# Block 0's first loads of an adapter and FFN kernel: x's first four k as two loads on two queues, B and A ahead of the rest of x

## The chip, the cores and the metric

The kernel runs on one core of a Trainium2 chip. The metric is the time of one execution on the device in microseconds (us), as the median of several runs. Engines are called by their names in the profile: PE (TensorE's products), PEld (its weight loads), DVE (VectorE), ACT (ScalarE), POOL (GpSimd) and SP (SyncE). SP does no arithmetic here. It issues most of the DMAs. ACTq and SPq are the queues of instructions of ScalarE and SyncE, in which register loads and DMA issues stand too.

## The reference

```python
def reference(x, ids, A, B, gate_w, up_w, down_w, ...):   # x: 8 x 256 x 1024
    Bx  = einsum('bni,bri->bnr', x, B[ids])               # rank 16, one adapter per batch row
    y   = einsum('bnr,bor->bno', Bx, A[ids])              # 8 x 256 x 1024
    q   = fp8(clip(y / in_scale)) * in_scale              # the same for gate and up
    h   = silu(q @ gate_w.T) * (q @ up_w.T)               # 2752 wide
    return x + fp8_linear(h, down_w)                      # back to 1024
```

x goes through a low-rank adapter that is picked by an index for each of the 8 batch rows, then through a feed-forward layer whose inputs are rounded to fp8, and is added at the end.

## The kernel before

The 2,048 tokens are worked on as four blocks t of 512 (two batch rows each), tokens along the free dimension. The 1,024 features of x are eight groups k of 128 partitions. x lies in memory in pieces, as `PIECES` says for each block: for block 0 the first piece holds k 0 to 3, the second k 4 to 6 and the third k 7, and each piece is one load (`load_x(t, k)`, line 378). Later blocks 2 and 3 come as one piece.

The head of the kernel is what the change touches. For block 0 TensorE does, in this order (lines 633 to 638):

- `pass_time(warm, 16, TB)`: 16 products of zeros, which need no load;
- `two_times_b(0, ...)`: Bx, tile `bx`, 8 groups k of four products each, with four more products of zeros behind k 3. All four products of a k read x's group k and one of the two adapters' B (tile `b`, two loads, one for each batch row);
- seven more products of zeros, while VectorE and ScalarE copy `bx` to `bm`;
- `two_times_a(0, bm)`: 64 products to the tiles `c`, from A (tile `a`, four loads of 16 rows each) and `bm`. VectorE and ScalarE round them to fp8, tile `xg`;
- `gate_up(0, 0, ...)`: the products `y` of the first chunk of 128 hidden features, from `xg` and the first chunk of weights (tile `w_gu`, 1 MB a chunk, the first as two halves). From here on products follow one another to the end: 22 chunks for four blocks, then the way back (`yd`).

TensorE's products are pinned in the order of the program (`multiply`, line 469). The adapter chosen for a batch row is a number in memory: `ids_i` is loaded first, and `adapter_of(batch, queue)` reads one number from it into a register of the queue that it names; a load of B or A that uses the number stands behind it on that queue.

All loads of data are issued by SyncE in the order of the program, but for `ids_i` and the first B, which ScalarE issues. In order of the program the loads are: ids; x k 0 to 3; B of batch row 0 (ScalarE); B of row 1; x k 4 to 6; A of row 1 (two loads); A of row 0 (two loads, behind another register load on SyncE); x k 7; five chunks of gate and up weights; then B, x and A of block 1, and B and x of blocks 2 and 3. ScalarE loads its activation table (`preload_act_table`, line 307) right behind the issue of ids.

The completion of each load is counted on a semaphore. The framework deals these out itself, and it adds the waits that follow from using one again.

Of the kernel before, what the change touches and what calls it, by code (L numbers as in the profile page):

```python
# [14 lines left out]
AF = mybir.ActivationFunctionType  # L15
# [10 lines left out]
NH = H // P  # L26
# [9 lines left out]

KS = NH // 2

PIECES = ((4, 3, 1), (4, 3, 1), (NH,), (NH,))
FP8_MAX = 448.0  # L40

SAME_MAX = 240.0
# [17 lines left out]
def x_of(x4, t, k):  # L60

    first = 0
    for n in PIECES[t]:
        if k < first + n:
            break
        first += n
    at = (t * NH + first) * P * TB
    piece = x4[at : at + n * P * TB].rearrange("(p k n) -> p k n", p=P, k=n)
    return piece, first
# [214 lines left out]
def adaln_ffn(  # L284
# [13 lines left out]
    nc = tc.nc  # L298
# [5 lines left out]

    ids_i = const.tile([1, NB], I32, name="ids_i")
    nc.scalar.dma_start(out=ids_i, in_=ids)
    nc.scalar.preload_act_table(AF.Silu)
    zeros = const.tile([P, TB], BF16, name="zeros")
    nc.vector.memset(zeros, 0.0)  # L309
    ones = const.tile([P, P], BF16, name="ones")  # L310
# [26 lines left out]
    with ExitStack() as fast:  # L337
# [5 lines left out]
        xs = [acts.tile([P, NH, TB], F32, name=f"x{t}") for t in range(NTB)]  # L343
# [8 lines left out]
        b_two = [lora.tile([P, 2 * BROW + R], F32, name=f"b{t}") for t in range(2)]  # L352
# [9 lines left out]
        def adapter_of(batch, queue):  # L362
            return queue.value_load(ids_i[0:1, batch : batch + 1], min_val=0, max_val=7)  # L363

        def load_b(b, i, adapter, queue):
            queue.dma_start(  # L366
                out=b[:, i * BROW : (i + 1) * BROW], in_=b8[bass.ds(adapter * P, P), :]
            )

        def load_a_two(t, j, adapter):  # L370
            for g in range(2):
                row = 32 * (2 * g + j) + R * j
                nc.sync.dma_start(  # L373
                    out=a_two[t][row : row + R],
                    in_=a8[bass.ds(adapter * 2 * R + g * R, R), :],
                )

        def load_x(t, k):
            piece, first = x_of(x4, t, k)
            ks = slice(first, first + piece.shape[1])  # L380
            nc.sync.dma_start(out=xs[t][:, ks, :], in_=piece)  # L381

        w_of = {}

        def load_gate_up(c, parts=1):
# [5 lines left out]
                nc.sync.dma_start(out=w[:, bass.ts(i, n)], in_=src[:, bass.ts(i, n)])  # L391
            w_of[c] = w

        load_x(0, 0)
        load_b(b_two[0], 0, adapter_of(0, nc.scalar), nc.scalar)
        second = adapter_of(1, nc.sync)
        load_b(b_two[0], 1, second, nc.sync)


        load_x(0, 4)  # L400
        load_a_two(0, 1, second)
        load_a_two(0, 0, adapter_of(0, nc.sync))
        load_x(0, 7)
        for c in range(NFIRST):
            load_gate_up(c, parts=1 if c else 2)
        adapters = [adapter_of(2 + q, nc.sync) for q in range(6)]
        for j in range(2):
            load_b(b_two[1], j, adapters[j], nc.sync)
        for k in (0, 4, 7):
            load_x(1, k)  # L410
        for j in range(2):
            load_a_two(1, j, adapters.pop(0))
# [5 lines left out]
        for q in range(4):  # L418
            nc.sync.dma_start(
                out=a_four[32 * q : 32 * q + R], in_=aT[bass.ds(adapters[q] * R, R), :]  # L420
# [309 lines left out]
        for k in range(NH - 1):  # L730
# [23 lines left out]
            first = k % 2 == 0  # L754
# [29 lines left out]
    with found_others.Else():  # L784

        k = NH - 1
# [9 lines left out]
        t, cols = NTB - 1, slice(cut, TB)  # L796
# [88 lines left out]
```

## Time and profile before

| what | value |
|---|---|
| median of 8 runs | 476.45 us (475.70 to 477.22) |
| the profiled execution's own time | 477.99 us |
| its span, first to last instruction | 476.2 us |
| mean granted clock of TensorE | 0.996 |
| TensorE busy | 470.4 us, 99% |
| VectorE, ScalarE busy | 105.6 us, 192.6 us |
| bytes moved by DMA | 53.44 MB, mean 112 GB/s |

The views have these forms. The chain of work that ended last is followed back from the last instruction to what released it, and it is listed in order of time: start, length, what ("issue" is time in which the engine waited for nothing that the profile shows). A timeline line gives start, length, engine, source line, operation, tile written and tiles read, and in brackets the idle time before it with what ended it. A line of the waits gives who waited for whom: total us, times, longest. A line of the windows gives, for a stretch of time, the busy time of each engine, the clock that was granted to TensorE, the share of the DMA engines and the rate. Several products can run beside one another in parts of TensorE's array, so the lengths of products are not summed, and their ends are modelled. When a wait is for several semaphores, the profile names the one that came last.

### The profile page before, as it was taken

How to read it: one execution, taken by the hardware profiler on the slowest of the kernel's cores; microseconds unless marked ns; L12 is line 12 of the kernel's file. 1: busy time of each engine (PE TensorE's matmuls, PEld its weight loads, DVE VectorE, ACT ScalarE, POOL GpSimd, SP SyncE). 2: the span in 40 equal slices, each digit the busy share in tenths (PEclk: the TensorE clock that was granted, in tenths of full speed). 3: DMA queues.
4: the chain of work that ended last, by engine and by line, in shares of the span. 5: the costliest groups of instructions: out<-in, count | busy, mean ns of one | idle time of the engine just before them, and what ended most of it. 6: DMA issues, size and time to landing. Idle time of an engine off the chain costs nothing.

```text
span 476.2 us, 6009 instructions
## 1 busy us (share of the span) xinstructions
PE 470.4 (99%) x2514; PEld 218.5 (46%) x2514; DVE 105.6 (22%) x163; ACT 192.6 (40%) x249; POOL 1.0 (0%) x7
## 2 busy tenths in 40 slices
PE   7999999999999999999999999999999999999997
PEld 4554544444444444444444444444444444444444
DVE  1323332122221212121221212132120121031031
ACT  1323346995556654433455453359212022021000
POOL 0000000000000000000000000000000000000000
PEclk9999999999999999999999999999999999999999
DMA  8996014522222112222201121123335255063031
GB/s 282 400 408 195 1 25 154 178 88 89 88 88 68 32 78 89 89 88 88 88 18 73 44 62 56 61 81 125 101 148 161 61 187 161 17 214 117 3 116 66
DMA packets 13780, 53.44 MB, mean 112 GB/s; under 512 B 1650, under 2 KB 2930, under 8 KB 10674
## 3 DMA queue, kind: packets, MB, share of 16 engines
q1 hardware_dynamic: 13600, 52.92, 32.2%
q8 instruction: 21, 0.34, 0.3%
q14 instruction: 13, 0.11, 0.1%
q10 hardware_dynamic: 146, 0.07, 0.0%
HBM read 44.60 MB, written 8.39 MB: 111 GB/s over the span
## 4 chain that ended last, share of the span: by engine, by line
PE 97%; DMA 1%; SPq 1%; issue 0%; DVE 0%
PE y L470 62%; PE yd L470 31%; PE c L470 2%; PE bx L470 1%; DMA x<-x 1%; SPq L373 0%; DMA ids_i<-ids 0%; SPq L363 0%; PE warm L470 0%; SPq L381 0%; SPq L366 0%; DVE o L695 0%; PE count L470 0%
## 5 line engine op out<-in xcount | busy, mean ns | idle before, releaser
L470 PE MATMUL y<-xg,w_gu 128*128 128x512 fp8e4 x1376 | 298.0, 379 | 0.0
L470 PEld LDWEIGHTS <-w_gu 128*128 128x128 bf16 x1376 | 134.2, 98 | 162.4 <-issue 1.3
L470 PE MATMUL yd<-hid,w_d 128*128 128x512 fp8e4 (+2 forms) x693 | 146.0, 373 | 0.0
L609 ACT ACTIVATE g<-y,gate_s 128x512 f32<-128x512 f32 (+1 forms) x88 | 59.9, 681 | 136.2 <-PE y L470 136.1
L610 DVE SCALAR_TENSOR_TENSOR hid<-y,up_by_down,g 128x512 fp8e4<-128x512 f32 x84 | 63.0, 750 | 219.5 <-PE y L470 161.4
L470 PEld LDWEIGHTS <-w_d 128*128 128x128 bf16 x693 | 66.6, 98 | 78.9 <-issue 1.7
L456 ACT ACTIVATE junk<-w_d 128x1408 bf16<-128x1408 uint16 (+1 forms) x16 | 21.2, 1323 | 88.3 <-DMA w_d<-w_d 88.2
L695 DVE SCALAR_TENSOR_TENSOR o<-yd,down_s,x 128x512 f32<-128x512 f32 x28 | 20.1, 748 | 107.4 <-PE yd L470 93.4
L456 ACT ACTIVATE junk<-w_gu 128x2048 bf16<-128x2048 uint16 (+1 forms) x22 | 41.0, 1864 | 0.0
L463 ACT ACTIVATE junk<-hid 128x2048 bf16<-128x2048 fp8e4 x21 | 40.0, 1905 | 0.4
L463 ACT ACTIVATE junk<-xg 128x2048 bf16<-128x2048 fp8e4 x8 | 15.3, 1911 | 0.2
L528 ACT ACTIVATE xg<-c,inv 128x512 fp8e4<-128x512 f32 x16 | 9.8, 686 | 9.8 <-PE c L470 9.8
L526 DVE TENSOR_SCALAR xg<-c,inv 128x512 fp8e4<-128x512 f32 x16 | 10.9, 745 | 3.9 <-PE c L470 3.9
L470 PE MATMUL warm<-zeros 128*128 128x512 bf16 (+1 forms) x27 | 6.2, 390 | 1.2 <-DVE zeros L309 1.2
L470 PE MATMUL bx<-x,b 128*32 128x128 f32 x128 | 4.4, 276 | 1.7 <-DMA x<-x 1.7
L695 DVE SCALAR_TENSOR_TENSOR o<-yd,down_s,xg 128x512 f32<-128x512 f32 (+2 forms) x5 | 3.2, 644 | 12.3 <-PE yd L470 12.3
L470 PE MATMUL c<-bm,a 32*128 32x128 f32 x128 | 5.5, 335 | 0.0
L470 PEld LDWEIGHTS c<-bm,a 32*128 32x128 f32 x128 | 5.1, 244 | 0.6 <-ACT bm L516 0.4
L516 ACT COPY bm<-bx 64x128 f32<-64x128 f32 x4 | 1.0, 261 | 10.3 <-PE bx L470 10.3
L470 PEld LDWEIGHTS bx<-x,b 128*32 128x32 f32 x128 | 3.4, 109 | 3.0 <-DMA x<-x 2.6
L470 PEld LDWEIGHTS <-zeros 128*128 128x128 bf16 x27 | 2.6, 117 | 4.2 <-issue 2.2
L456 ACT ACTIVATION_READ_ACCUMULATOR junk<-w_gu 128x1 f32 x22 | 4.2, 193 | 0.0
(47 smaller groups left out, 41.9 us busy)
## 6 DMA issues: line engine op xcount, KB each, us to landing
w_gu<-w_gu SPq DMA_DIRECT2D x20, 1024.0 KB, 4.8
outT<-o SPq DMA_DIRECT2D x31, 256.0 KB, 2.2
w_d<-w_d SPq DMA_DIRECT2D x8, 704.0 KB, 5.1
w_d<-w_d SPq DMA_DIRECT2D x8, 640.0 KB, 3.9
x<-x SPq DMA_DIRECT2D x2, 2048.0 KB, 11.0
x<-x SPq DMA_DIRECT2D x2, 1024.0 KB, 8.0
x<-x SPq DMA_DIRECT2D x2, 768.0 KB, 8.9
w_gu<-w_gu SPq DMA_DIRECT2D x3, 512.0 KB, 4.9
```

Of the source, the lines that this page charges most:

```text
L456: nc.scalar.activation(junk_like(w), low(w), AF.Copy, accum_out=lows[:rows, column : column + 1])
L463: nc.scalar.activation(junk_like(q), q, AF.Square, accum_out=squares[:rows, column : column + 1])
L470: tc.keep_in_program_order(nc.tensor.matmul(*args, **kwargs))
L516: copy(bm[64 * to : 64 * (to + 1), other], bx[half][64 * half : 64 * (half + 1)],)
L526: nc.vector.tensor_scalar(to, c, scale, None, ALU.mult, saturate=False)
L528: nc.scalar.activation(to, c, AF.Copy, scale=scale, saturate=False)
L609: nc.scalar.activation(g[rows], gates, AF.Silu, scale=gate_s[: gates.shape[0]])
L610: nc.vector.scalar_tensor_tensor(to, in0=ups, scalar=up_by_down[rows], in1=g[rows], op0=ALU.mult, op1=ALU.mult, saturate=False,)
L695: nc.vector.scalar_tensor_tensor(o, in0=y, scalar=down_s, in1=x, op0=ALU.mult, op1=ALU.add)
```

## The change

`PIECES` of block 0 becomes (2, 2, 3, 1) and that of block 1 (7, 1), so x lies in memory in other pieces. For block 0, k 0 and 1 are loaded by SyncE and k 2 and 3 by ScalarE, behind ids. The table load of ScalarE comes behind that. B of batch row 0 and now A of row 0 are loaded by ScalarE, B and A of row 1 by SyncE, and x's k 4 to 6 and k 7 follow on SyncE. The second register load of row 0's adapter, on SyncE, goes away. Block 1's x comes in two loads, not three.

```diff
-PIECES = ((4, 3, 1), (4, 3, 1), (NH,), (NH,))
+PIECES = ((2, 2, 3, 1), (7, 1), (NH,), (NH,))
...
     nc.scalar.dma_start(out=ids_i, in_=ids)
-    nc.scalar.preload_act_table(AF.Silu)
...
-        def load_a_two(t, j, adapter):
+        def load_a_two(t, j, adapter, queue=nc.sync):
             for g in range(2):
                 row = 32 * (2 * g + j) + R * j
-                nc.sync.dma_start(
+                queue.dma_start(
                     out=a_two[t][row : row + R],
                     in_=a8[bass.ds(adapter * 2 * R + g * R, R), :],
                 )
 
-        def load_x(t, k):
+        def load_x(t, k, queue=nc.sync):
             piece, first = x_of(x4, t, k)
             ks = slice(first, first + piece.shape[1])
-            nc.sync.dma_start(out=xs[t][:, ks, :], in_=piece)
+            queue.dma_start(out=xs[t][:, ks, :], in_=piece)
...
         load_x(0, 0)
-        load_b(b_two[0], 0, adapter_of(0, nc.scalar), nc.scalar)
-        second = adapter_of(1, nc.sync)
+        load_x(0, 2, nc.scalar)
+        nc.scalar.preload_act_table(AF.Silu)
+        first, second = adapter_of(0, nc.scalar), adapter_of(1, nc.sync)
+        load_b(b_two[0], 0, first, nc.scalar)
         load_b(b_two[0], 1, second, nc.sync)
-
-
+        load_a_two(0, 0, first, nc.scalar)
+        load_a_two(0, 1, second)
         load_x(0, 4)
-        load_a_two(0, 1, second)
-        load_a_two(0, 0, adapter_of(0, nc.sync))
         load_x(0, 7)
         for c in range(NFIRST):
             load_gate_up(c, parts=1 if c else 2)
...
-        for k in (0, 4, 7):
+        for k in (0, 7):
             load_x(1, k)
```

## The prediction

> **What bounds the kernel now.** I read the page's busy table first, then the chain of work that ended last, then TensorE's own timeline at the start.
>
> ```profile
> PE 470.4 (99%) x2514; PEld 218.5 (46%) x2514; DVE 105.6 (22%) x163; ACT 192.6 (40%) x249; POOL 1.0 (0%) x7
> ```
>
> TensorE is busy for 99% of the span, so only what happens before its unbroken run can be won. The chain shows where that run begins (columns: start in us, length in us, what):
>
> ```profile
> 6.61 3.55 DMA x<-x
> 10.16 0.04 issue
> 10.21 0.43 PE bx L470 x8
> 10.63 0.75 PE warm L470 x7
> 11.38 3.32 PE c L470 x64
> 14.70 16.51 PE y L470 x76
> ```
>
> Up to 10.16 us the end is set by SyncE's issues and by one load: x's last k of block 0, issued at 6.61 and landed at 10.16. From 14.70 us on the chain is TensorE to the end. A microsecond won before 14.70 us is a microsecond of the total, until some later load comes too late. TensorE's timeline from 5 to 15 us shows the steps of the head:
>
> ```profile
> 6.09 1.17 PE L470 MATMUL bx<-x,b 128*32 128x128 f32 x32
> 7.20 0.40 PE L470 MATMUL warm<-zeros 128*128 128x128 bf16 x4
> 8.41 0.86 PE L470 MATMUL bx<-x,b 128*32 128x128 f32 x24 [0.82 <-DMA x<-x]
> 10.21 0.43 PE L470 MATMUL bx<-x,b 128*32 128x128 f32 x8 [0.93 <-DMA x<-x]
> ```
>
> There are two gaps, 7.60 to 8.41 us (until k 4 to 6 land) and 9.27 to 10.21 us (until k 7 lands). The first product starts at 6.09 us: x's first piece has landed at 0.75 + 4.9 = 5.65 us (the DMA issues give 4.9 us), the two B at 2.87 + 3.1 = 5.97 and 2.91 + 3.2 = 6.11 us, and the 16 warm products end about there too. The windows view has a third cost (columns: window and its us, then busy us and count of PE, PEld, DVE, ACT, POOL, then granted clock, DMA share, GB/s):
>
> ```profile
> 3.90:7.31 3.41, 3.41 (x45) 1.83 (x43) 0.51 (x6) 0.00 (x0) 0.00 (x0) 1.00 1.00 393
> 7.31:10.72 3.41, 1.66 (x39) 1.02 (x38) 0.05 (x1) 0.00 (x0) 0.00 (x0) 1.00 0.92 281
> 10.72:14.13 3.41, 3.41 (x59) 3.21 (x61) 1.18 (x3) 1.23 (x4) 0.00 (x0) 0.50 1.01 328
> ```
>
> After a window in which TensorE was busy for 1.66 of 3.41 us, it ran at half clock for 3.41 us. The 64 products c took 3.32 us there; the chain has the same 64 of block 1 at 2.07 us. That is 1.25 us.
>
> **The change, part by part.**
>
> *x's first four k on two queues.* Bytes are the same: 128 packets of 8,192 B at 309 ns become 256 of 4,096 B at 159 ns (durations of the trace's DMA packets; the second from the w_gu halves), over 16 engines 2.54 for 2.47 us, +0.07 us. What can be won is the slow start: from 2 to 4 us the DMA moved 307 GB/s, from 14.13 to 17.55 us 422, so at most 2 x 115 / 422 = 0.55 us; at least nothing. I take 0.25. By itself this brings TensorE nothing: the first 32 products still wait for the warm ones and for B (6.09 us), and have until the next piece lands.
>
> The Trainium skill ("DMA: Bandwidth & Descriptors", section "Issuing engines are not separate DMA queues") says that DMAs of different issuing engines run on the same 16 DMA engines and interleave, so that two queues save only the time to issue. The share of 0.85 at 2 to 4 us against 1.00 later leaves some room beside that rule; by it the 0.25 us would be nothing, and the sum below 0.25 us worse.
>
> *ScalarE's queue.* It issues one x load (about 0.42 us) before the table load, and two A loads behind B. Its next work is the copy at 10.72 us, after 8.1 us of waiting, so the two A loads (about 0.6 us each) are hidden; A is needed only at 11.31 us. The table load moves from 1.30 to about 1.75 us and ends at 3.03. The register load of the adapter ran at 1.93 us inside the table load, so B should still go at 2.87 us: no cost. From above: if it did wait, B goes 1.1 us later and lands at 7.1; the first 32 products then end at 8.3 us, still before the next piece. It is that piece that hides all of this.
>
> *SyncE's queue.* A's two remaining loads now stand ahead of k 4 to 6, and one register load (0.5 us) and two A loads go. This is the row:
>
> ```profile
> 2.91 0.37 SPq L366 DMA_DIRECT2D b<-b  x1
> 3.32 0.45 SPq L381 DMA_DIRECT2D x<-x  x1
> 3.99 2.58 SPq L373 DMA_DIRECT2D a<-a  x4
> 6.61 0.42 SPq L381 DMA_DIRECT2D x<-x  x1
> 7.08 4.10 SPq L391 DMA_DIRECT2D w_gu<-w_gu  x6
> ```
>
> With 0.6 us for each A, SyncE is free for k 4 to 6 at 3.28 + 1.16 = 4.44 instead of 3.32 us, and for k 7 at 4.9 instead of 6.61 us.
>
> But there is a wait that the diff does not show. SyncE's waits up to 30 us:
>
> ```profile
> SPq L373 <- DMA w_gu<-w_gu: 5.5, 3, 2.0
> SPq L391 <- DMA x<-x: 0.4, 1, 0.4
> ```
>
> No data joins an A load to w_gu, or w_gu to x. Counting loads in program order (ids, x, B, B, x, four A, x, w_gu, w_gu, then this w_gu), the w_gu load at 8.39 us is the 13th and was held until the 5th, x's k 4 to 6, had landed at 8.37; each A load of block 1 that waits stands eight behind the w_gu load it waits for. So at most eight loads are under way, and each waits for the landing of the one eight before. In the changed order ids, x, x, B, B and four A come first; k 4 to 6 is the tenth and waits for x's first half, k 7 the eleventh and waits for the second half.
>
> The first half lands between 4.5 us (alone: 3.55 us for 256 KB at 6.61 and 4.9 us for 1,024 KB give 4.0 for 512 KB, less 0.25) and 5.65 us (sharing every engine evenly with the other half). I take 4.9, as it is issued 0.55 us ahead. Issue to first packet was 1.0 us for the first x, so k 4 to 6 begins at 5.9 us; in the profile it began at about 5.4 (behind B) and landed at 8.37, 3.0 us later. So it lands at **8.9**, 0.5 us later than now; A's 64 packets of 84 ns (0.34 us over 16 engines) go in the time before it. The bounds: 8.3 (start gain full, no hold) and 9.65 (first half at 5.65).
>
> k 7 follows at once: 128 packets of 84 ns, 0.67 us, landing at **9.6** instead of 10.16. Its late issue, which the second gap came from, is gone.
>
> *TensorE then.* k 4 to 6 start 0.05 us after landing and take 0.86 us, to 9.8 us; k 7 has landed, 0.43 us more, end about **10.3** instead of 10.63: 0.3 us won, between -0.4 (9.65 + 1.38 = 11.0) and +1.0.
>
> *The clock.* The gaps of 0.81 + 0.94 us become one of 1.35 (7.60 to 8.95). If the next window falls as in the profile, TensorE is busy about 2.06 of 3.41 us instead of 1.66. The trace has dropped clocks after 1.66 and kept them after 3.41, and nothing between: worth nothing to 1.25 us in a run that loses the clock now. I take 0.15 over the runs.
>
> The same skill ("TensorE: Matmul & The Clock Gate", "HAM oscillation") warns of idle gaps over about 3.4 us. Here no gap is over 0.95 us and the clock fell, so the row decides; by the rule neither kernel would lose any. That page also calls the window free-running, which one trace cannot show.
>
> *x of block 1 in two loads.* One issue of 0.47 us goes. k 0 to 6 lands when k 4 to 6 did, 16.87 + 12.8 = 29.7 us; its first use is at 31.21, so it is hidden by 1.5 us, and w_gu's earlier issues move it forward too. If that cover went, TensorE would wait at 31 us by what is missing. The first w_gu half lands by 11.95 us now, before 12.7, the earliest that y could start; the third w_gu load was held until 8.39 and is not now.
>
> *Sum.* 0.3 + 0.15 = 0.45 us. The profiled execution took 477.99 us (span 476.2 and 1.8 around it); it would take 477.69, or 476.4 if its clock stays. The median shown is 476.45, 1.54 below it, so most timed runs seem to lose less clock than the profiled one. From the median: **476.0**.
>
> **Rivals.**
>
> *The gap closes fully (faster).* The start gain is full, k 4 to 6 lands at 8.3 and k 7 at 9.0: products end at 8.3 + 0.05 + 0.86 + 0.43 = 9.64, 1.0 us won, and a gap of 0.75 us keeps the clock in the runs that lose it now (1.25 us in about a third: 0.4; a window of 3.41 us holds both gaps whole if it begins between 6.80 and 7.60 us, a quarter of all places, and much of both a little beside that). 475.0. For it: the DMA's share of 0.92 and 281 GB/s from 7.31 to 10.72 us. Against it: the hold. What is then late next is w_gu's third load (8.39 + 8.8 = 17.2 us now).
>
> *The hold takes the place of the gap (slower).* The halves land together at 5.65 us and the queue runs dry. By 4.45 us for 768 KB (between the 3.55 and 4.9 above) k 4 to 6 lands at 10.1 and the products end at 11.5: 0.85 us lost, and a gap of 2.5 us halves the clock in more runs, 1.25 in a third: 0.4. 477.7. It decides from a landing of k 4 to 6 at 9.25 us on (10.63 less 1.38), an issue after 5.2 us.
>
> *It does nothing.* The halves run as the whole did, the bytes end when they ended, B and A cost what k 7 gains: 476.4.
>
> **How the numbers follow.** Likeliest case 0.48, 476.0 (its own range 475.5 to 476.4); gap closed 0.27; nothing 0.12; hold 0.13, of which 0.03 stays within bounds. A measurement of this kernel tells about 0.2% (0.95 us) from no change. Faster 0.27, same 0.48 + 0.12 + 0.03 = 0.63, slower 0.10. The range, 474.7 to 477.2, leaves out the outer halves of the first and third rival.
>
> **What the new profile would show.** Right: k 4 to 6 issued near 4.9 us, waiting on x; TensorE's products of k 7 directly behind those of k 6, ending at 10.0 to 10.6. Wrong: that issue at 4.44 with no wait; a gap still ahead of k 7; half clock at other places; a wait for w_gu or x after 14 us. The prediction fails most easily by when x's first half lands, and by what the clock does in the timed runs.

## The result, and the profile after

The changed kernel takes 477.94 us (median of 12 runs, 477.34 to 478.93); the kernel before took 476.67 us beside it (33 runs). The ratio is 1.003, with an interval of 1.0021 to 1.0039: 0.3% or 1.27 us **slower**. The prediction was 476.0 us, with 477.2 us as its upper end. The profiled execution took 477.62 us (span 475.8 us). Fast executions are compared throughout; one of a later kernel (e13), at 549.51 us with a granted clock of 0.852, is left out of its median and ratio.

The chain of work that ended last, of the changed kernel (start, length, what):

```profile
1.30 6.43 DMA x<-x
7.73 0.02 issue
7.75 0.36 SPq L380
...
9.11 8.55 DMA w_gu<-w_gu
17.66 0.05 issue
17.71 13.12 PE y L472 x60
```

Before, the chain went from SyncE's A loads through x's last load to the products. Now it starts with x's half on ScalarE's queue, issued at 1.30 and landed at 7.73 us. SyncE issues k 7 (line 380) only then. The weights stand behind k 7 on that queue, and the third load of weights, the second chunk, lands at 17.66 us. The first 16 products y are not in the chain any more: TensorE waits for the second chunk.

Why the half took so long is in SyncE's timeline:

```profile
0.74 0.86 SPq L380 DMA_DIRECT2D x<-x  x2
...
7.75 0.36 SPq L380 DMA_DIRECT2D x<-x  x1
8.15 2.92 SPq L390 DMA_DIRECT2D w_gu<-w_gu  x6
```

The first line has **two** x loads. The second of them, at 1.19 us, is k 4 to 6, which the program has behind A. In the kernel as built it stands in the time in which SyncE waits for ids. So 1.75 MB of x were under way before the first B was issued at 2.88 us. That made the half later, but is not all of its 6.43 us: without the early k 4 to 6 the half took 5.41 us in e1 and 4.18 in e6 below. SyncE issued its B and its two A next (the lines left out), and then nothing from 4.43 to 7.75 us; its waits up to 30 us say for what (us in total, times, longest):

```profile
SPq L372 <- DMA w_gu<-w_gu: 5.9, 4, 2.0
SPq L380 <- DMA x<-x: 3.3, 1, 3.3
```

TensorE's timeline from 5 to 20 us shows both costs:

```profile
8.59 1.08 PE L472 MATMUL bx<-x,b 128*32 128x128 f32 x32 [0.98 <-DMA a<-a]
9.61 0.40 PE L472 MATMUL warm<-zeros 128*128 128x128 bf16 x4
9.93 1.08 PE L472 MATMUL bx<-x,b 128*32 128x128 f32 x32
10.95 0.56 PE L472 MATMUL warm<-zeros 128*128 128x128 bf16 x7
11.44 2.18 PE L472 MATMUL c<-bm,a 32*128 32x128 f32 x64
13.57 3.61 PE L472 MATMUL y<-xg,w_gu 128*128 128x512 fp8e4 x16
17.71 2.55 PE L472 MATMUL y<-xg,w_gu 128*128 128x512 fp8e4 x11 [0.52 <-DMA w_gu<-w_gu]
```

The two B landed at 8.30 and 8.46 us (before at about 6), so the first product starts at 8.59 instead of 6.09 us. The two gaps of before are gone (9.93 follows 9.61), but this one late start is worth more than both. The last line is the wait for the second chunk. The windows at the same places as before:

```profile
7.31:10.72 3.41, 2.43 (x66) 1.86 (x68) 0.51 (x6) 0.00 (x0) 0.00 (x0) 1.00 0.57 206
10.72:14.13 3.41, 3.41 (x86) 2.72 (x79) 2.02 (x5) 2.02 (x5) 0.00 (x0) 1.00 0.97 345
```

The clock stays at 1.00, and `c` takes 2.18 us. But the DMA engines are busy for 0.57 of the first window (0.92 before) and move 206 GB/s (281 before); by microsecond, from 7.5 to 9.5 us:

```profile
7.50:8.50 1.00, 0.11 (x1) 0.00 (x0) 0.02 (x1) 0.00 (x0) 0.00 (x0) 1.00 0.13 39
8.50:9.50 1.00, 0.91 (x32) 0.84 (x32) 0.49 (x6) 0.00 (x0) 0.00 (x0) 1.00 0.36 119
```

The queue ran dry while SyncE was held. From the start of the second chunk to the end of the span it takes 458.1 us (475.8 less 17.71), and so it does in the kernel before (474.7 less 16.56, below). So here the head alone decides, and it is read by when the second chunk's products start.

The execution profiled before the change was an unusual one. The kernel before, profiled again (476.47 us, span 474.7), has this chain:

```profile
6.62 3.26 DMA x<-x
...
10.84 2.11 PE c L470 x63
12.95 3.58 PE y L470 x16
...
16.56 13.12 PE y L470 x60
```

`c` takes 2.11 us here, not 3.32: no clock is lost. In 105 later runs of that kernel the mean granted clock was 0.996 twice. Against this execution the changed kernel's products y start at 13.57 instead of 12.91 us (0.66 us, B is late), and the wait for the weights puts 0.49 us on top: 17.71 less 16.56 is **1.15 us**, of the 1.27 measured.

### The profile page after: what moved, and what is told of

It is laid out like the page before. It is cut to its first block, busy times and chain, and to the rows that moved or that the text cites. A ratio compares the mean times of both kernels' runs of the same rounds, so it can differ in the third digit from the quotient of the medians.

```text
span 475.8 us, 6006 instructions
## 1 busy us (share of the span) xinstructions
PE 470.3 (99%) x2514; PEld 217.3 (46%) x2514; DVE 105.6 (22%) x163; ACT 192.4 (40%) x249; POOL 1.0 (0%) x7
## 3 DMA queue, kind: packets, MB, share of 16 engines
HBM read 44.60 MB, written 8.39 MB: 111 GB/s over the span
## 4 chain that ended last, share of the span: by engine, by line
PE 96%; DMA 3%; SPq 0%; ACTq 0%; DVE 0%; issue 0%
PE y L472 62%; PE yd L472 31%; DMA w_gu<-w_gu 2%; DMA x<-x 1%; PE c L472 1%; PE bx L472 1%; SPq L390 0%; ACTq L306 0%; SPq L380 0%; DVE o L697 0%; PE count L472 0%
## 5 line engine op out<-in xcount | busy, mean ns | idle before, releaser
L472 PE MATMUL warm<-zeros 128*128 128x512 bf16 (+1 forms) x27 | 7.4, 440 | 1.2 <-DVE zeros L308 1.2
L472 PE MATMUL c<-bm,a 32*128 32x128 f32 x128 | 4.3, 277 | 0.0
L472 PEld LDWEIGHTS c<-bm,a 32*128 32x128 f32 x128 | 3.9, 186 | 0.5 <-ACT bm L518 0.4
```

What stands on the lines that cost most here:

```text
L472: tc.keep_in_program_order(nc.tensor.matmul(*args, **kwargs))
```

## The experiments

Three theories stood against one another. *Order:* the early issue of k 4 to 6 is the whole cost, and the change in its written order would be as fast as forecast. *Queue:* the second queue for x is the cost. *Hold and dry queue:* the limit of eight loads under way leaves the DMA engines without work, wherever B and A come first. Times are medians; each ratio is to the kernel before in the same runs.

### The order that the change writes (e1, e5, e7)

**e1_pinned**: the changed kernel, SyncE's loads kept in the order of the program.

```diff
-            queue.dma_start(out=xs[t][:, ks, :], in_=piece)
+            load = queue.dma_start(out=xs[t][:, ks, :], in_=piece)
+            if queue is nc.sync:
+                tc.keep_in_program_order(load)
...
```

The loads of weights are kept in the same way (not shown).

> The changed kernel with SyncE's loads pinned to the order of the program: k 4 to 6 goes out behind B and A, no longer second on SyncE. Order theory (the changed kernel lost time because k 4 to 6 was issued at 1.19 us, ahead of B and A, which put B and A 2.3 us later and k 7 and the weights 1.1 us later): B lands near 6 us, the first product starts near 6.1, k 7 is issued before 6 us, the second chunk of weights lands before 17 us, and the time is that of the prediction, 476.0 (475.5 to 476.5). Queue theory (two queues, smaller packets and A on ScalarE cost by themselves): the time stays at 477.5 to 478.2.

478.28 us, ratio 1.004 (1.0025 to 1.0055). The order theory fell: the written order is no better. This median stands between two groups: three of the six executions kept the clock (477.48 to 477.72 us, 0.7 us or more above the kernel before) and three had a mean of 0.996 (478.84 to 479.43). Its chain:

```profile
4.46 5.98 DMA x<-x
10.44 0.04 issue
10.48 1.08 PE bx L476 x32
```

B and A did come first (B landed by 7.15 us), and k 4 to 6 was issued at 4.46 us without a hold (x's first half had landed at 3.97), but it took 5.98 us to land. The prediction had put its landing at 8.9.

**e5_after_one_queue**: the changed kernel with all of x on SyncE, which kept the written order by itself.

```diff
-        load_x(0, 2, nc.scalar)
+        load_x(0, 2)
```

> The changed kernel with x's k 2 and 3 issued by SyncE behind k 0 and 1, not by ScalarE; with two issues SyncE keeps the written order, so k 4 to 6 goes out behind B and A. It is the pinned run (478.3 us) with one queue for x. Queue theory (x's half on ScalarE's queue costs): 476.5 to 477.0. Dry-queue theory (k 4 to 6 behind B and A comes when the DMA engines have run out of bytes, and its first packets are slow): as the pinned run, 477.6 to 478.4, with k 4 to 6 landing after 9.5 us.

479.0 us, 1.0043 (1.003 to 1.0055); four of the six executions, the profiled one among them, had a clock of 0.996, the other two took 477.96 and 478.39 us. k 4 to 6 was issued at 4.45 and landed at 10.93 us. So the second queue is not what makes it late: the queue theory fell as the whole cost.

**e7_before_ba_first**: the kernel before with x's first piece whole, and B and A on two queues ahead of the rest of x, SyncE's loads kept in that order as in e1.

```diff
-        load_b(b_two[0], 0, adapter_of(0, nc.scalar), nc.scalar)
-        second = adapter_of(1, nc.sync)
+        first, second = adapter_of(0, nc.scalar), adapter_of(1, nc.sync)
+        load_b(b_two[0], 0, first, nc.scalar)
         load_b(b_two[0], 1, second, nc.sync)
-        load_x(0, 4)
+        load_a_two(0, 0, first, nc.scalar)
         load_a_two(0, 1, second)
-        load_a_two(0, 0, adapter_of(0, nc.sync))
+        load_x(0, 4)
```

> The kernel before with the other part alone: x's first piece as one load, B and A on two queues right behind it, then k 4 to 6 and k 7 (pinned). Queue theory: no x on ScalarE, so 476.0 to 476.9, k 7 issued near 5.7 instead of 6.6 us. Dry-queue theory: k 4 to 6 is issued at 4.45 instead of 3.3 us, as B and A end, so it lands after 9 us and the time is 477.2 to 478.2.

477.55 us, 1.0018 (1.0007 to 1.0029); k 4 to 6 issued at 4.45, landed at 10.02 us. The windows from 5.5 to 6.5 us of the kernel before (the repeated profile), of e1 and of e7, in that order (the last two columns are the DMA share and GB/s):

```profile
5.50:6.50 1.00, 1.00 (x14) 0.45 (x15) 0.50 (x6) 0.00 (x0) 0.00 (x0) 1.00 1.04 421
```
```profile
5.50:6.50 1.00, 1.00 (x6) 0.41 (x5) 0.00 (x0) 0.00 (x0) 0.00 (x0) 1.00 0.95 154
```
```profile
5.50:6.50 1.00, 1.00 (x6) 0.33 (x4) 0.29 (x5) 0.00 (x0) 0.00 (x0) 1.00 0.90 218
```

A high share with few GB/s means slow packets. Those of k 4 to 6 took 628 ns (median) in this microsecond in e1, 731 in e5 and 410 in e7, against 234 ns when the engines have work queued. k 4 to 6 was issued at 4.45 us, and its first packets ran at 5.7 to 5.8 us, when little of the loads ahead was left: the start of its transfer was paid in the open. x's first piece, which starts in the kernel before with nothing ahead of it, shows the same (958 ns for the packets of 1.5 to 2.5 us, median, and 309 ns from 3 us on, repeated profile). Why first packets are slow, the runs do not show.

### Parts alone (e2, e3, e4, e6)

**e2_before_k4_first**: the kernel before with k 4 to 6 right behind x's first piece, ahead of B. This is meant to make B late and nothing else.

```diff
         load_x(0, 0)
+        load_x(0, 4)
...
-        load_x(0, 4)
         load_a_two(0, 1, second)
```

> The kernel before with one part alone: k 4 to 6 is issued right behind x's first piece, ahead of B and A. Order theory in its simple form (late B and A are the loss): first product at 8 us instead of 6.1, time 477.5 to 478. Order theory in its second form (the loss is k 7 and the weights issued late, since the load eight places before k 7 had to land at 7.73 us): here the load eight places before k 7 is x's first piece, landed by 5.7 us, so the weights are issued as before and the time is 476.4 to 476.9 although B is late. Queue theory: nothing to expect, 476.6.

476.88 us, 1.0007 (0.9998 to 1.0016): no difference that can be told. B landed at 8.25 and 8.5 us, as late as in the changed kernel, and the weights were held for it, to 8.26 us. But k 7 was not held: issued at 6.12, it landed at 9.47 us, and from 7.5 to 8.5 us the engines moved 266 GB/s (39 in the changed kernel). The second chunk landed at 17.07 us, and TensorE reached it without a stop at 17.13, 0.57 us later than in the repeated profile of before. So late B costs at most some 0.8 us here, by the interval.

**e3_after_k7_free**: the changed kernel with k 4 to 6 and k 7 right behind x's half, so that k 7 is not held.

```diff
         load_x(0, 2, nc.scalar)
+        load_x(0, 4)
+        load_x(0, 7)
```

> The changed kernel with k 7 written right behind k 4 to 6, both ahead of B and A, so that k 7 is not held by the landing of x's second half. Second form of the order theory: the DMA engines don't run dry from 7.7 to 9.6 us, the weights go out near 7.4 instead of 8.15 us, and the time is 476.9 to 477.4. Simple form (late B and A): B and A land near 9 us, 0.6 later than in the changed kernel, and the time is 478.0 to 478.6.

477.9 us, 1.0027 (1.0016 to 1.0039). The hold only moved: SyncE's last A load was held to 7.86 us by the same half, which landed at 7.84, and the weights behind it went from 8.22 us. But TensorE did not wait for these: the second chunk landed at 16.60 us, and y ran from 14.50 us without a stop. What made it late is the first product, at 8.96 us, with B and A behind all of x; the time is 0.1 us below what was expected if late B and A are the loss. The miss shows that the limit counts loads, whichever stands in that place.

**e4_before_x1_two**: the kernel before with block 1's x in two loads, the change's `(7, 1)`.

> The kernel before with block 1's x in two loads (k 0 to 6, k 7) instead of three, and nothing else. All forms of the order theory: no change, 476.4 to 476.9. If this part costs, through a wait of TensorE for x of block 1 near 31 us: 477 or more.

476.54 us, 0.9999 (0.9989 to 1.0008): that part is free, as forecast.

**e6_before_x_two_queues**: the kernel before with x's first piece alone split on two queues, as in the change, and SyncE's loads in the order of the program (kept as in e1).

```diff
-PIECES = ((4, 3, 1), (4, 3, 1), (NH,), (NH,))
+PIECES = ((2, 2, 3, 1), (4, 3, 1), (NH,), (NH,))
...
-    nc.scalar.preload_act_table(AF.Silu)
...
         load_x(0, 0)
+        load_x(0, 2, nc.scalar)
+        nc.scalar.preload_act_table(AF.Silu)
```

> The kernel before with one part alone: x's first four k as two loads on SyncE's and ScalarE's queues, the table load behind that, and everything else in the old order (k 4 to 6 behind B, A behind it; SyncE's loads pinned to it). Queue theory: 477.4 to 478.2. Dry-queue theory and order theory: k 4 to 6 is issued at 3.3 us while the engines have bytes, so the time is that of before, 476.4 to 476.9.

477.19 us, 1.0012 (1.0003 to 1.0021): 0.45 us slower, between what the queue theory (477.4 or more) and the others (476.9 or less) expected. Its profiled run was its fastest (476.27 us), with k 7 at 9.46 us, so the trace doesn't show where the 0.45 us go in the others. That stays open.

### The changed kernel again, and without the holds (e8, e9, e10)

**e8_after_again**: the changed kernel, profiled once more.

> The changed kernel again, for a second trace. Both theories: 477.3 to 478.9 as in its timed runs; it shows whether the chain again ends the head with the wait for the second chunk of weights, and whether TensorE's clock falls in the head in some runs.

477.77 us. Again x's half lands late (7.89 us), k 7 is issued behind it at 7.90 us, and the second chunk starts at 17.78. The picture is that of the first profile.

**e9_after_a_gpsimd**: the changed kernel with A of block 0 issued by GpSimd. GpSimd's loads aren't among the eight, so k 7 and the weights are not held.

```diff
-        load_a_two(0, 0, first, nc.scalar)
-        load_a_two(0, 1, second)
+        load_a_two(0, 0, adapter_of(0, nc.gpsimd), nc.gpsimd)
+        load_a_two(0, 1, adapter_of(1, nc.gpsimd), nc.gpsimd)
```

> The changed kernel with A of block 0 issued by GpSimd, whose loads don't count among the eight of SyncE and ScalarE; k 7 and the weights are then held by nothing before 8 us. Dry-queue theory: the engines have bytes from 7.5 to 9.5 us, the second chunk of weights lands before 17 us, TensorE waits for late B and A alone (second chunk of products from 17.1 us), and the time is 476.7 to 477.3. If late B and A are the whole loss, or the second queue is: as the changed kernel, 477.7 to 478.2.

477.41 us, 1.001 (1.0 to 1.002), 0.1 us above the upper end. k 7 was issued at 3.48 us, the weights from 4.04, and the second chunk had landed at 15.14 us. The first product still waited for B (8.65 us), and y ran from 13.78 us without a stop. With GpSimd's loads the first loads go 0.13 us later (0.88 for 0.74 us), which the expectation didn't have. The second chunk's products begin at 17.18 us instead of 17.71. The span's end is 0.4 us further behind VectorE's last instruction (2.9 for 2.5); e6, e14 and e15 have 2.8 to 2.9 too, without GpSimd, so this can't be put down to it.

**e10_before_a_gpsimd**: the kernel before with the same edit.

> The kernel before with only A of block 0 issued by GpSimd: k 7 goes out at 3.8 instead of 6.6 us and the weights from 4.3 us, with no load ahead held. Dry-queue theory: k 7 lands before 9 us, the second chunk of weights before 16.3, and the time is 475.6 to 476.3, below both kernels. If issue times and dry engines are not what the head waits for: 476.5 to 476.9.

477.88 us, 1.0023 (1.0011 to 1.0034): a miss. A, issued by GpSimd at 5.48, landed at 11.36 us, and `c` waited 0.93 us for it. B had landed by 6.40 us, but TensorE still ran the products of zeros, and the first product came at 7.21. So this pair can't price the holds.

### A alone, and taken out (e13, e14, e15)

**e13_before_a_scalar**: the kernel before, with A of row 0 moved to ScalarE behind its B; k 4 to 6 stays right behind B.

```diff
-        load_b(b_two[0], 0, adapter_of(0, nc.scalar), nc.scalar)
+        first = adapter_of(0, nc.scalar)
+        load_b(b_two[0], 0, first, nc.scalar)
         second = adapter_of(1, nc.sync)
...
         load_x(0, 4)
+        load_a_two(0, 0, first, nc.scalar)
         load_a_two(0, 1, second)
-        load_a_two(0, 0, adapter_of(0, nc.sync))
```

SyncE's loads are kept in the order of the program, as in e1.

> The kernel before with A of batch row 0 issued by ScalarE behind its B and nothing else moved: k 4 to 6 stays right behind B, k 7 goes out when x's first piece has landed, near 5.7 instead of 6.6 us, and the weights from 6.2 us. Dry-queue theory: k 7 lands near 9.3 instead of 9.9, the second chunk of weights before 16.3 us, time 476.0 to 476.6, the fastest of all. If a ScalarE queue beside SyncE's costs by itself: 477 or more.

475.98 us (median of 11), 0.9984 (0.9975 to 0.9994): **faster than both**. Its chain:

```profile
3.33 5.20 DMA x<-x
...
12.42 16.52 PE y L475 x76
```

SyncE is relieved of a register load and two A loads, so k 7 goes at 5.64 us (held until x's first piece has landed at 5.62) and is no longer in the chain; k 4 to 6, issued at 3.33 us as before, is the bound. This is the part of the change that wins, by 0.71 us. In the change it was tied to an order that lost more.

**e14_after_no_a** and **e15_before_no_a**: the changed kernel and the one before, both without the four loads of A for block 0. This frees the eight of four loads in both.

> The changed kernel without the four A loads of block 0 (its output for block 0 is left wrong by that): only four loads fewer, so that k 7 and the first weights are held by nothing. If the hold makes half of the loss and late B the other: TensorE reaches the second chunk at 16.9 to 17.2 us, limited by B, time 476.8 to 477.2. If late B and A are all: 477.7 to 478. If the hold is all: 476.2 to 476.6.

> The kernel before without the four A loads of block 0 (left out as in the run beside it), the partner of that run. With no load held and 128 KB fewer: k 7 lands near 9 us, the second chunk of weights before 16 us, TensorE reaches the second chunk near 16 us, time 475.7 to 476.3. The difference to its partner is then the price of late B alone with no hold, 0.6 to 1.2 us; under 0.4 would say that late B costs little and the hold is the loss.

477.01 us, 1.0003 (0.9994 to 1.0012), and 475.9 us, 0.9979 (0.997 to 0.9988). e14 has no dry stretch; from 7.5 to 9.5 us:

```profile
7.50:8.50 1.00, 0.25 (x2) 0.02 (x1) 0.10 (x1) 0.00 (x0) 0.00 (x0) 1.00 1.09 426
8.50:9.50 1.00, 0.99 (x32) 0.82 (x32) 0.41 (x6) 0.00 (x0) 0.00 (x0) 1.00 1.00 385
```

Its second chunk lands at 13.89 us; TensorE starts at 8.51, when B has landed, and y runs without a stop. Of the chains, e14's goes by B, e15's by the weights:

```profile
2.92 5.45 DMA b<-b
...
13.50 16.56 PE y L470 x76
```
```profile
5.29 10.38 DMA w_gu<-w_gu
15.67 0.05 issue
15.72 13.12 PE y L468 x60
```

Without A the changed kernel takes 0.93 us less (477.94 to 477.01). That is the holds, and with them A's 128 KB; e9, which keeps A's bytes, takes 0.53 us less. The 1.11 us between e14 and e15 go with B being late, by the chains (with earlier weights e15 would be faster still, and it would be more); what the split of x costs by itself, as in e6, is not parted from this. And e15 wins 0.79 us over the kernel before, much like e13: that is what A's loads there cost, their issue and register load on SyncE, their places and their bytes. So the way from before to after has three steps: without A, -0.79; B late, +1.11; A's loads back, on two queues, in the places that hold k 7 and the weights, +0.93. That these add up to +1.25 us says nothing by itself, as each step starts where the last one ends. But the traces agree with them: the second chunk's products start at 16.56 us in the kernel before, at 15.72 in e15, 16.95 in e14 and 17.71 in the changed kernel, which makes -0.84, +1.23 and +0.76. Another order of the steps would give other prices: in e2, where A stays in the kernel before, late B costs 0.13 us by the medians and 0.57 by the traces.

### Is it the dry queue? (e11, e16, e12)

**e11_pinned_w_first**: e1 with the first half of the first chunk of weights right behind x's first half, so that the engines have bytes while k 4 to 6 starts.

```diff
         load_x(0, 2, nc.scalar)
+        load_gate_up(0, 2, (0,))
```

> The pinned changed kernel (478.3 us) with the first half of the first chunk of weights, 512 KB that are needed anyway, issued right behind x's first half, so that the engines still have bytes when k 4 to 6 is issued. Dry-queue theory: k 4 to 6 lands earlier than in the pinned run (10.4 us) although 512 KB more stand ahead of it, 9.2 to 9.9 us, and the time is 476.8 to 477.6. If the bytes ahead decide: k 4 to 6 lands 1.2 us later, near 11.6, and the time is 479 or more.

479.97 us, 1.0061 (1.0038 to 1.0084). It decides nothing: with one load more ahead, k 4 to 6 itself was held until x's half landed at 7.23 us. Issued at 7.25, it landed 4.30 us later.

**e16_ba_first_w_ahead**: the same in e7, with that half right behind x's first piece.

> The run with B and A on two queues behind x's first piece (477.55 us; k 4 to 6 landed at 10.0), with the first half of the first weights, 512 KB, issued right behind x's first piece, so that the DMA engines have bytes until about 7 us. Dry-queue theory: k 4 to 6, issued when x's first piece has landed, lands no later than before, 9.5 to 10.1 us, though 512 KB more stand ahead, and the time is 476.7 to 477.4. If the bytes ahead decide: it lands near 11.2 us and the time is 478 or more.

478.22 us, 1.0046 (1.0028 to 1.0064). k 4 to 6, held to 5.73 us, landed at 10.20: 0.18 us later than in e7 although 512 KB more stood ahead of it and it was issued 1.28 us later. For the landing the dry queue theory had 9.5 to 10.1 us, and bytes alone 11.2, so it speaks for the first, though it lies 0.1 us outside. The time speaks for neither: B now landed at 7.92 us, k 7 was held for it to 7.93 and landed at 11.32.

**e12_before_again** is the repeated profile of the kernel before that was shown with the result.

> The kernel before again, for a second trace. If the profiled execution of before (477.99 us, clock 0.996) was an unusual one: k 7 lands before 9.8 us, the clock does not fall in the head, and the time is 476 to 477. If it was usual: the clock falls at about 10.7 us again.

476.47 us: no clock lost, k 7 landed at 9.88 us (9.8 at the latest was expected).

## Why the prediction was wrong, point by point

**The step that failed first** is the order of issues: "In the changed order ids, x, x, B, B and four A come first; k 4 to 6 is the tenth". The trace has k 4 to 6 as SyncE's second load, at 1.19 us, landed at 7.33. So B and A, which the forecast took for early, were the late ones, and no rival had this. "k 4 to 6 issued near 4.9 us, waiting on x" was wrong. k 7 was to go at 4.9 us and went at 7.75. The runs price this at 1.11 us for late B and up to 0.93 for the holds, against 0.79 won.

**The second step would have failed without the first.** "So it lands at **8.9**, 0.5 us later than now" stood on the 3.0 us that k 4 to 6 had needed behind other bytes. In the written order it landed at 10.44 (e1), 10.93 (e5) and 10.02 us (e7): with 5.6 to 6.5 us from issue to landing, as its start wasn't hidden any more. There was no hold of it either: x's first half, put at 4.5 to 5.65 us, landed at 3.97 (e1), and k 4 to 6 went at 4.46 with no wait, a sign of being wrong that the text had named. The third rival had 4.45 us for this and a landing of 10.1; its form was right, and its price of 4.45 us was 4.30 in e11, where k 4 to 6 was held as that rival had it. But it blamed the halves that land together, and gave it 0.13.

**The base was too favourable.** The gap of 0.93 us ahead of k 7 and the 1.25 us of half clock were read from one execution, and in the repeated profile they are 0.74 us and nothing. The text saw that the median lay 1.54 us lower, and still took 0.15 us for the clock and gave 0.27 to a rival that had 0.4 us from it.

**What held.** The limit of eight loads, read from two lines of the waits, shows in nearly every run: k 7, eleventh in the program, waited for x's second half as the text said, but that half landed at 7.73 us instead of 5.65 at the latest, with k 4 to 6 beside it on the engines. "What is then late next is w_gu's third load (8.39 + 8.8 = 17.2 us now)" was the right place (17.66 us), though the text had it in its faster case. Block 1's x in two loads is free (e4). ScalarE's issues are hidden: its B went at 2.88 us, table load or not. For the two queues the text took 0.25 us of gain; e6 has 0.45 us of loss. The row decides for the rule that the prediction weighed (the Trainium skill, "DMA: Bandwidth & Descriptors", "Issuing engines are not separate DMA queues"): no gain beyond the time to issue. The loss is more than that rule tells.

**The rival that came nearest** is the hold that takes the place of the gap, at k 7 and the weights, not at k 4 to 6: 477.7 us forecast, 477.94 measured. That the numbers lie so close is luck: it added 0.85 us for a landing of k 4 to 6 at 10.1 us (it landed at 7.33) and 0.4 for a clock that was not lost.

**What stays open**: whether it is the dry queue alone that makes the first packets of k 4 to 6 slow in e1, e5 and e7 (e16's landing speaks for it, e11 didn't separate), why the kernel as built has k 4 to 6 so early, when e5 with one load more on SyncE does not, and e6's 0.45 us.

## What to carry to other kernels

Read the order of issues from the trace of the built kernel, not from the source: a load that needs no index can stand ahead of loads that wait for one, as k 4 to 6 did in the changed kernel, e9 and e14, but not in the kernel before or e5. Then count the loads under way, and for each later one ask which landing it waits for; small loads that are cheap in bytes still take places, and whatever stands behind them on the queue, weights too, pays. A big load moved behind small ones should still be issued while bytes ahead of it run; otherwise its start is paid in the open, and in e1, e5 and e7 that cost more than an earlier issue of B and A gained.

## What the runs showed of the hardware

- Busy DMA engines may move little: 154 GB/s at a share of 0.95 (e1, 5.5 to 6.5 us) against 421 at 1.04 in the kernel before. The same 768 KB landed 4.3 us after the issue (e11) or 6.5 (e5).
- The granted clock fell to 0.996 or less in 3 of 6 runs of e1, 4 of 6 of e5, 5 of 6 of e11 and 3 of 11 of e7, whose profiles have one wait of 1.9 to 2.9 us for k 4 to 6, and in 4 of 12 of e16, against 2 of 105 of the kernel before. In e1 such a run took 1.1 to 2.0 us more than one that kept its clock. A share of work at which it falls can't be read from this: with 1.66 us of work from 7.31 to 10.72 us the clock was lost next (before), with 1.53 (e1) and 1.37 (e7) it was kept.
- The same 16 products of zeros at the start ended at 7.62 us in one profile of the changed kernel and at 6.78 in the other (6.13 and 6.32 before), with nothing to wait for.
- With loads issued by GpSimd the first loads went 0.13 us later (e9, e10). A then took 5.2 to 5.9 us from issue to landing, about what x's k 4 to 6 and k 7, issued by SyncE at that time, took (5.2 and 5.6, e10).
